# A two-layer graph network on one core: norm work one operation per gap, factor steps between halves of projections, the first two tiles ahead of the second burst

## Chip, core and metric

The kernel runs on one core of one Trainium2 chip. The metric is the device time of one execution in microseconds (us). PE is TensorE, DVE is VectorE, ACT is ScalarE, POOL is GpSimd, SP is SyncE, which here only issues DMAs.

## What is computed

The input x has 8 batches of 2048 nodes with 256 features, all in float32, and one 2048 x 2048 adjacency matrix that all batches share. Two layers follow each other.

```python
# layer 0: 4 heads of 64; the keys in 8 chunks of 256, softmax within each chunk
q, k, v = x @ Wq.T + bq, x @ Wk.T + bk, x @ Wv.T + bv
scores = clip(q kc / 8, -10, 10);  scores = where(adj == 0, -10, scores)
ctx    = sum over chunks of softmax(scores within the chunk) @ vc
x = layernorm(x + (layernorm(ctx @ Wo.T + bo + x) * gamma + beta))
# layer 1: graph attention, 4 heads of 64
Wh = x @ W;  e[i, j] = leaky_relu(s_src[i] + s_dst[j], 0.2), -inf where adj == 0
x = layernorm(x + elu(softmax over j (e) @ Wh))
```

## The kernel before

**Staging.** The adjacency matrix is turned once, during batch 0, into two tables in DRAM: clipD (int8, clip bounds of layer 0) and edgeD (bf16, the mask of layer 1). Then the kernel goes through the batches. In the loop over batch b, layer 0 of batch b and layer 1 of batch b - 1 (`lower`, called `along` where it runs) are woven together by hand[...].

**The pair loop.** A batch has 64 slots (4 query groups q x 2 head pairs x 8 chunks), taken in 32 pairs p. With QP = 8 pairs to a query group, i = p % 8 is the place in the group. In pair p, PE gets in this order: `burst(p + 1)`, four units of scores for the next pair (line 398, tile ps, 32 matmuls); one `use` of layer 1 (line 884, tile pa); `product(s0)` (line 449, tile pc); three more `use`; `product(s1)`; and in some pairs half of an output projection (line 600, `LAST_OF`) or of the layer 1 projection (line 642, `NEXT_LAST`). DVE gets: the reciprocal of the slot before (line 466, in `normalize`), the evictions of two units (line 415, tile pr), two tiles e (line 855, in `make`), the middle steps, the reciprocal of s0, two more evictions and two more tiles e. ACT takes the exponentials (line 438) and copies the products out (line 456); POOL scales and adds them up (lines 473, 475).

**The tables of steps.** The norm work of layer 0 for a group of 512 nodes is an object `Between`. Its steps are bias (line 584), shift (588), add (611), scale (617) and again (620) on DVE, and sums, squares and apply on ACT. `FIRST_OF`, `MIDDLE_OF`, `LAST_OF` and `FINALLY_OF` say at which i the current group does which step: at the head of the pair, in the middle, after the second product, and at the end. `NEXT_MIDDLE`, `NEXT_LAST` and `NEXT_FINALLY` say it for the group before. `turn_context` (line 493) transposes a block of the context on DVE. `CLOSING` says at which pair the output norm of batch b - 2 does what: load (line 956), add (959), sums, squares, factors, finish.

**PSUM.** `two_banks` gives out three tiles of two banks in turn (ps, pc, po, pw, pp, pv and others), so a tile waits for the readers of the third one before it. `one_bank` gives out two single banks, where the accumulators pa of layer 1 stand during the pair loop.

**The transition.** Between the pair loops of two batches, `order` lists the pieces: the projections of the next batch (k0, v0, q0 to k3, v3, q3; chunk g in each), the last group's norm and its layer 1 projection, the three factor steps `fs` (most, spread, rows), which turn the layer 1 scores into factors, `coming.start` (loads the first row of scores, srow), and `start_next` (burst 0 with its evictions). The tiles e of layer 1 read srow and an edge tile each (four edge buffers, three loaded ahead). All loads stand on SP's one queue in program order.

## Time and profile before

| | us |
|---|---|
| median of 3 runs | 3708.56 |
| lowest and highest run | 3708.34, 3709.61 |
| profiled execution, its own time | 3715.49 |
| span of the profiled execution | 3713.7 |
| PE busy | 3547.3 (96%) |
| DVE busy | 3055.2 (82%) |
| ACT busy | 2302.6 (62%) |
| POOL busy | 1458.7 (39%) |
| mean granted TensorE clock | 0.991 of full speed |

The span is the time from the first to the last instruction of the profiled execution; all times of single instructions and waits below are of that one execution. In a row of waits stand the total in us, how often, and the longest. In a row of the timeline stand the start, the duration, the engine, the line of the kernel, the operation, what is written and read, the shape and the count; in brackets stands how long the engine was idle before it and what released it.

### The profile page before, as it was taken

What the parts mean: (1) busy time and instruction counts of PE and PEld (TensorE: products, weight loads), DVE (VectorE), ACT (ScalarE), POOL (GpSimd) and SP (SyncE); (2) the same over time, 40 slices, a digit from 0 to 9 for tenths busy, and PEclk for the clock granted to TensorE, in tenths of its full rate; (3) what the DMA queues carried; (4) which work ended last, traced back from release to release, by engine and by line L of the source; (5) the groups of instructions that cost most, each with busy time, mean ns of one, the idle gap of its engine ahead of it and who ended that gap; (6) DMA issues with size and microseconds to landing.
All of it is one profiled execution on the core that took longest, in us unless ns stands there. A gap on an engine that the chain in (4) does not pass through costs nothing.

```text
span 3713.7 us, 169348 instructions
## 1 busy us (share of the span) xinstructions
PE 3547.3 (96%) x76884; PEld 2630.8 (71%) x76884; DVE 3055.2 (82%) x3652; ACT 2302.6 (62%) x4119; POOL 1458.7 (39%) x1259
## 2 busy tenths in 40 slices
PE   8999999999999999999999999999999999998777
PEld 5666677776777677776777767777677776775677
DVE  5886689978889699896989969988689977896787
ACT  4786456655666566665666656666566665666376
POOL 0454233333333334333433423434333333334366
PEclk9999999999999999999999999999999999999998
DMA  7764344554545455554555545555455554543432
GB/s 184 169 138 84 107 142 140 149 120 144 155 137 147 99 170 151 151 145 104 163 150 143 141 121 167 145 147 126 130 149 145 148 131 138 150 143 95 142 119 90
DMA packets 692866, 512.33 MB, mean 138 GB/s; under 512 B 429616, under 2 KB 528304, under 8 KB 692144
## 3 DMA queue, kind: packets, MB, share of 16 engines
q1 hardware_dynamic: 642144, 467.80, 46.1%
q10 hardware_dynamic: 50000, 33.70, 2.9%
q8 instruction: 601, 9.85, 1.1%
q14 instruction: 121, 0.99, 0.1%
HBM read 440.27 MB, written 61.08 MB: 135 GB/s over the span
## 4 chain that ended last, share of the span: by engine, by line
PE 65%; DVE 15%; issue 4%; ACT 2%; DMA 1%; POOL 1%; DVEq 0%; ACTq 0%; SPq 0%; POOLq 0%
PE pa L884 19%; PE pc L449 18%; PE ps L398 16%; DVE pr L415 6%; DVE e L855 5%; PE pp L342 4%; PE pw L642 3%; PE po L600 3%; PE pv L358 2%; DMA et<-edgeD 1%; DVE h L928 1%; DVE qT L493 1%; DVE xg L588 0%; DVE y L620 0%; ACT raw L456 0%
## 5 line engine op out<-in xcount | busy, mean ns | idle before, releaser
L438 ACT ACTIVATE pr<-pr 128x1024 f32<-128x1024 f32 x960 | 994.8, 1054 | 449.7 <-DVE pr L415 381.8
L415 DVE SCALAR_TENSOR_TENSOR pr<-ps,slab 128x1024 f32<-128x1024 f32 x960 | 1116.5, 1204 | 127.8 <-PE ps L398 104.2
L855 DVE SCALAR_TENSOR_TENSOR e<-srow,gd,et 128x1024 f32<-128x1024 f32 x896 | 1175.4, 1344 | 22.7 <-PE pa L884 9.0
L884 PEld LDWEIGHTS pa<-waug,e 128*64 128x64 f32 x32768 | 1014.1, 140 | 240.3 <-issue 183.4
L884 PE MATMUL pa<-waug,e 128*64 128x65 f32 x32768 | 1067.5, 224 | 61.8 <-DVE e L855 42.9
L449 PE MATMUL pc<-vaug,pr 128*64 128x65 f32 x30720 | 994.6, 222 | 48.9 <-DVE pr L415 23.3
L449 PEld LDWEIGHTS pc<-vaug,pr 128*64 128x64 f32 x30720 | 944.6, 138 | 78.2 <-DVE pr L415 40.6
L398 PE MATMUL ps<-qT,kT 64*64 64x512 f32 x8192 | 951.7, 598 | 13.5 <-DVE pr L415 10.9
L473 POOL TENSOR_TENSOR part<-raw,rd 128x512 f32<-128x512 f32 x448 | 473.5, 1057 | 1232.3 <-DVE rd L466 1228.5
L398 PEld LDWEIGHTS ps<-qT,kT 64*64 64x64 f32 x8192 | 285.4, 132 | 501.0 <-issue 272.4
L456 ACT COPY raw<-pc 128x520 f32<-128x520 f32 x512 | 302.9, 592 | 537.3 <-PE pc L449 536.0
L475 POOL TENSOR_TENSOR acc<-acc,part 128x512 f32<-128x512 f32 x448 | 593.9, 1326 | 35.2
L466 DVE RECIPROCAL rd<-raw 128x8 f32<-128x8 f32 x512 | 99.6, 194 | 195.8 <-ACT raw L456 192.1
L473 POOL TENSOR_TENSOR acc<-raw,rd 128x512 f32<-128x512 f32 x64 | 66.8, 1044 | 362.0 <-DVE rd L466 362.0
L642 PE MATMUL pw<-w_sb,x1T 128*64 128x264 f32 (+1 forms) x800 | 125.1, 392 | 6.5 <-DVE x1T L300 5.0
L600 PE MATMUL po<-wo_sb,qT 128*64 128x256 f32 (+1 forms) x912 | 120.7, 381 | 1.6 <-DVE rd L466 0.8
L342 PE MATMUL pp<-xT,wk_sb 128*128 128x512 f32 x256 | 118.8, 608 | 2.5 <-DVE xT L312 1.3
L342 PE MATMUL pp<-xT,wq_sb 128*128 128x512 f32 x256 | 117.7, 603 | 0.0
L358 PE MATMUL pv<-wv_sb,xT 128*128 128x256 f32 x512 | 117.4, 382 | 0.0
L920 ACT ACTIVATE sums<-sums,dn 128x64 f32<-128x64 f32 x448 | 117.1, 334 | 0.4 <-ACT y L564 0.4
L826 POOL TENSOR_TENSOR e<-e,et 128x1024 f32<-128x1024 f32 x42 | 90.0, 2146 | 48.4 <-ACT e L825 39.6
L642 PEld LDWEIGHTS pw<-w_sb,x1T 128*64 128x64 f32 (+1 forms) x800 | 83.7, 153 | 33.8 <-issue 5.3
(140 smaller groups left out, 2567.5 us busy)
## 6 DMA issues: line engine op xcount, KB each, us to landing
et<-edgeD SPq DMA_DIRECT2D x896, 256.0 KB, 3.5
slab<-clipD SPq DMA_DIRECT2D x256, 256.0 KB, 4.3
srow<-rowD SPq DMA_DIRECT2D x64, 512.0 KB, 5.1
xg<-in_x_dram SPq DMA_DIRECT2D x32, 512.0 KB, 5.5
x1D<-y ACTq DMA_DIRECT2D x32, 512.0 KB, 3.0
ctxD<-acc ACTq DMA_DIRECT2D x56, 256.0 KB, 3.9
ctx<-ctxD SPq DMA_DIRECT2D x224, 64.0 KB, 4.0
xp<-in_x_dram SPq DMA_DIRECT2D x224, 64.0 KB, 2.5
```

The source lines that it names most:

```text
L342: nc.tensor.matmul(pps[c], lhsT=w[:, kc, c * P : (c + 1) * P], rhs=st["xT"][:, kc, :], start=(kc == 0), stop=(kc == KC - 1),)
L398: nc.tensor.matmul(ps[z * D : (z + 1) * D, k, :], lhsT=kT[rows, hp, t * P + z * D : t * P + (z + 1) * D], rhs=qT[rows, hp, cols], start=Tr ...
L415: nc.vector.scalar_tensor_tensor(pr, ps, -CLIP, row.unsqueeze(1).to_broadcast([P, 2, CH]), op0=ALU.max, op1=ALU.min,)
L438: nc.scalar.activation(pr, pr, AF.Exp, scale=0.125)
L449: nc.tensor.matmul(pc[z * D : (z + 1) * D, k, to], lhsT=probs[s][u][:, k, i * P + z * D : i * P + (z + 1) * D], rhs=vaug[:, KT * c + u, 2 ...
L456: nc.scalar.copy(raws[s].rearrange("p k i d -> p k (i d)"), pc[:, :, : QT * D1])
L473: nc.gpsimd.tensor_mul(part, raw[:, :, :, :D], rd.to_broadcast([P, 2, QT, D]))
L475: nc.gpsimd.tensor_add(accv, accv, part)
L600: nc.tensor.matmul(po[z, k, :], lhsT=qT[:, c, t * P + z.start : t * P + z.stop], rhs=wo_sb[:, c, :], start=(c == 0), stop=(c == KC - 1),)
L642: nc.tensor.matmul(pw[z, k, : F + 2 * H], lhsT=self.x1T[:, c, u * P + z.start : u * P + z.stop], rhs=w1_sb[:, c, :], start=(c == 0), stop= ...
L855: nc.vector.scalar_tensor_tensor(e, row, self.gd[:, h, j : j + 1], self.mask(k), op0=ALU.max, op1=ALU.mult,)
L884: nc.tensor.matmul(self.pa[i // QT][z * D : (z + 1) * D, i % QT, :], lhsT=e[:, i * P + z * D : i * P + (z + 1) * D], rhs=self.waug[:, j, h ...
```

## The change

Four edits. The tables of steps: bias moves from i = 2 to 1; shift from the middle of i = 6 to the head of i = 6, the factors stay; scale moves from i = 0 of the next group to i = 7 of its own; again moves to i = 0, and the sums and squares of the second norm move one pair earlier with it; the context transpose of i = 6 moves to the head of i = 7. The closing table: all four loads stand at the batch start, and the adds are at pairs 0, 3, 1 and 7 for groups 0 to 3. The transition: `linear` takes a step to run between its two halves; the factor steps stand inside k3, after it, and inside q2, with one-bank tiles (but in the last batch); v3 comes directly ahead of `start_next`, the exponentials of pair 0 come ahead of q3, and the first two tiles of layer 1 (`coming.make` twice) come at the end of the transition. In pair 0 the two `make` that stood after burst 1 are gone.

```diff
--- before.py
+++ after.py
@@ -331,13 +331,15 @@
             else:
                 st["xT"] = transposed(st["x"], "xT", nc.vector.tensor_copy)
 
-        def linear(dst, w, bias, apart=False):
+        def linear(dst, w, bias, apart=False, between=None):
             if apart:
                 pps = [one_bank([P, CH], "pp") for _ in range(KC)]
             else:
                 pp = two_banks([P, KC, CH], "pp")
                 pps = [pp[:, c, :] for c in range(KC)]
             for c in range(KC):
+                if c and between:
+                    between()
                 for kc in range(KC):
                     nc.tensor.matmul(
                         pps[c],
@@ -370,9 +372,9 @@
         return [
             load,
             turn,
-            lambda: linear(kT, wk_sb, bk_sb),
+            lambda between=None: linear(kT, wk_sb, bk_sb, False, between),
             values,
-            lambda: linear(qT, wq_sb, bq_sb, b > 0 and g == NCH - 1),
+            lambda between=None: linear(qT, wq_sb, bq_sb, b > 0 and g == NCH - 1, between),
         ]
 
 
@@ -660,10 +662,12 @@
     FIRST_OF = {
         3: lambda o: o.add((0, 1)),
         4: lambda o: o.add((2, 3)),
+        6: lambda o: o.shift(),
     }
     MIDDLE_OF = {
-        2: lambda o: o.bias(),
-        6: lambda o: (o.a.factors(), o.shift()),
+        1: lambda o: o.bias(),
+        6: lambda o: o.a.factors(),
+        7: lambda o: o.scale(),
     }
     FINALLY_OF = {
         4: lambda o: o.a.sums(every),
@@ -675,15 +679,14 @@
         3: lambda o: o.output((2, 3)),
     }
     NEXT_MIDDLE = {
-        0: lambda o: o.scale(),
-        1: lambda o: o.again(),
+        0: lambda o: o.again(),
         3: lambda o: o.b2.factors(),
         4: lambda o: o.load(),
         5: lambda o: o.turn(),
     }
     NEXT_FINALLY = {
-        1: lambda o: o.b2.sums(every),
-        2: lambda o: o.b2.squares(every),
+        0: lambda o: o.b2.sums(every),
+        1: lambda o: o.b2.squares(every),
         3: lambda o: o.finish(),
     }
     NEXT_LAST = {
@@ -701,16 +704,17 @@
         ed = small.tile([P, H, NT], F32, tag="ed", name="ed", bufs=1)
         gd = small.tile([P, H, NT], F32, tag="gd", name="gd")
         st = {}
+        banks = one_bank if b + 1 < B else two_banks
 
         def most():
             nc.vector.tensor_reduce(top, d, AX.X, ALU.max)
-            pt = two_banks([P, CH], "pt")
+            pt = banks([P, CH], "pt")
             nc.tensor.transpose(pt[:H, :P], top, identf)
             st["most"] = small.tile([H, 1], F32, tag="most", name="most")
             nc.vector.tensor_reduce(st["most"], pt[:H, :P], AX.X, ALU.max)
 
         def spread():
-            pb = two_banks([P, CH], "pb")
+            pb = banks([P, CH], "pb")
             nc.tensor.matmul(
                 pb[:, :H],
                 lhsT=st["most"].to_broadcast([H, P]),
@@ -729,7 +733,7 @@
 
         def rows():
 
-            pr = two_banks([P, CH], "pr1")
+            pr = banks([P, CH], "pr1")
             nc.tensor.transpose(pr[: H * NT, :P], s.rearrange("p h t -> p (h t)"), identf)
             flat = small.tile([H * NT, P], F32, tag="flat", name="flat", bufs=1)
             nc.scalar.copy(flat, pr[: H * NT, :P])
@@ -1066,16 +1070,16 @@
             finish_constants()
 
     CLOSING = {
-        -1: [(0, "load", HOME), (1, "load", HOME)],
+        -1: [(0, "load", HOME), (1, "load", HOME), (2, "load", HOME_Y), (3, "load", HOME_Y)],
         0: [(0, "add"), (0, "sums")],
-        1: [(0, "squares")],
-        2: [(1, "add"), (0, "factors"), (0, "finish"), (2, "load", HOME_Y)],
-        3: [(1, "sums")],
-        4: [(1, "squares"), (3, "load", HOME_Y)],
-        5: [(2, "add"), (1, "factors"), (1, "finish")],
+        1: [(2, "add"), (0, "squares")],
+        2: [(0, "factors"), (0, "finish")],
+        3: [(1, "add"), (1, "sums")],
+        4: [(1, "squares")],
+        5: [(1, "factors"), (1, "finish")],
         6: [(2, "sums")],
-        7: [(2, "squares")],
-        8: [(3, "add"), (2, "factors"), (2, "finish")],
+        7: [(3, "add"), (2, "squares")],
+        8: [(2, "factors"), (2, "finish")],
         9: [(3, "sums")],
         10: [(3, "squares")],
         11: [(3, "factors"), (3, "finish")],
@@ -1142,6 +1146,8 @@
                 turns[0].pop(0)()
 
             hook(FIRST_OF, {})
+            if i == QP - 1:
+                turn_context(q, 0)
             if p:
                 normalize(s0 - 1)
             if more:
@@ -1151,9 +1157,6 @@
                 exps(*us[0])
                 exps(*us[1])
             if along:
-                if p == 0:
-                    for _ in range(STEP):
-                        along.make()
                 along.rest(1)
                 along.make()
                 along.use()
@@ -1169,8 +1172,6 @@
                 closing.do(p, "add", "factors")
             if i == 2 and q:
                 turn_context(q - 1, 1)
-            if i == QP // 2 + 2:
-                turn_context(q, 0)
             product(s0)
             if along:
                 normalize(s0)
@@ -1200,7 +1201,6 @@
             if p == PAIRS - 1:
                 if b + 1 < B:
                     turns[0].pop(0)()
-                group.scale()
                 group.again()
             product(s1)
             if along and more:
@@ -1260,8 +1260,9 @@
             order = [begin, early[0], *rest, l1, k0, ctx, early[2], v0, steps[0], *rest, steps[1], t1, l2, *rest]
             order += [q0, steps[2], early[3], steps[3], l3, k1, *rest, steps[4], v1, early[4], t2, q1]
             order += [steps[5], k2, steps[6], early[5], early[6], steps[7], coming.begin, v2, t3]
-            order += [lambda: [load_slab(p) for p in range(2)], steps[8], steps[9], k3, fs[0], q2, fs[1]]
-            order += [v3, fs[2], coming.start, start_next, q3, lambda: [exps(*us) for us in units_of(0)]]
+            order += [lambda: [load_slab(p) for p in range(2)], steps[8], steps[9]]
+            order += [lambda: k3(fs[0]), fs[1], lambda: q2(fs[2]), coming.start, v3, start_next]
+            order += [lambda: [exps(*us) for us in units_of(0)], q3, coming.make, coming.make]
         else:
 
             step = lower.step
```

## Prediction, made before the changed kernel ran

> **What bounds the kernel now.** I read the page first, then the waits of TensorE, then the timeline around a batch start and around one pair. A "pair" p is one turn of the loop of 32 pairs in a batch, i = p % 8.

> ```profile
> PE 3547.3 (96%) x76884; PEld 2630.8 (71%) x76884; DVE 3055.2 (82%) x3652; ACT 2302.6 (62%) x4119; POOL 1458.7 (39%) x1259
> ```

> TensorE is nearly always occupied, so only its stalls can be won. VectorE at 82% is the engine that could cause them. The waits of PE say so (total us, times, longest):

> ```profile
> PE pa L884 <- DVE e L855: 42.9, 23, 6.3
> PE pc L449 <- DVE pr L415: 23.3, 44, 1.2
> PE pc L449 <- issue: 22.5, 32, 2.3
> PE pa L884 <- issue: 11.9, 16, 1.8
> PE ps L398 <- DVE pr L415: 10.9, 23, 2.9
> PE pt L499 <- POOL acc L475: 10.8, 8, 5.6
> ```

> Three rows are VectorE being late (77 us), two are PE's own issue. The change speaks to the first kind. Where are they? At the start of batch 2 the timeline shows:

> ```profile
> 856.54 2.47 DVE L855 SCALAR_TENSOR_TENSOR e<-srow,gd,et 128x1024 f32<-128x1024 f32 x2
> ...
> 857.96 1.15 PE L884 MATMUL pa<-waug,e 128*64 128x65 f32 x32 [1.19 <-DVE e L855]
> ...
> 858.93 0.68 DVE L928 SCALAR_TENSOR_TENSOR h<-ee,sums 128x512 f32<-128x512 f32 x1
> ...
> 861.92 1.22 DVE L959 TENSOR_TENSOR h<-h,x1g 128x1024 f32<-128x1024 f32 x1
> ...
> 864.49 1.70 PE L449 MATMUL pc<-vaug,pr 128*64 128x65 f32 x51 [0.71 <-DVE pr L415]
> ```

> The reader is to see that the first tile e is made only after two evictions of burst 1, PE waits 1.19 us for it, and VectorE, then behind, costs 0.71 us more at pc. The waits asked in a window over each batch start repeat it: 1.2 us in all seven (batches 1 to 7), 0.7 us in the six that also close an older batch (0.6 in one).

> Inside a batch, pairs 14 and 15 of batch 3 on VectorE:

> ```profile
> 1474.24 0.71 DVE L928 SCALAR_TENSOR_TENSOR h<-ee,sums 128x512 f32<-128x512 f32 x1
> ...
> 1477.41 1.21 DVE L588 TENSOR_TENSOR xg<-xg,beta_sb 128x1024 f32<-128x1024 f32 x1
> 1478.55 0.70 DVE L493 STREAM_TRANSPOSE qT<-ctx 128x512 f32<-128x512 f32 x1
> 1479.18 0.16 DVE L466 RECIPROCAL rd<-raw 128x8 f32<-128x8 f32 x1
> ...
> 1490.44 0.20 DVE L466 RECIPROCAL rd<-raw 128x8 f32<-128x8 f32 x1 [1.09 <-ACT raw L456]
> ```

> and on PE:

> ```profile
> 1480.48 2.31 PE L449 MATMUL pc<-vaug,pr 128*64 128x65 f32 x64 [0.25 <-DVE pr L415]
> 1482.72 2.81 PE L398 MATMUL ps<-qT,kT 64*64 64x512 f32 x24
> 1485.68 1.09 PE L398 MATMUL ps<-qT,kT 64*64 64x512 f32 x8 [0.15 <-DVE pr L415]
> ```

> Pair 15 has no norm work, and there VectorE idles 1.09 us before the reciprocal of slot s0: that is the middle gap, and it holds one operation of 1.2 us. Pair 14 put 2.2 us into it (factors, shift, context transpose), after an L928, so the second product starts late, and the next burst breaks after 24 of 32 matmuls because the first eviction is late. From the starts of the 32 ps matmuls a pair lasts 11.21 us undisturbed, 12.94 with half an output projection, 12.99 with half of the layer 1 projection.

> [...] the trace has 1207 to 1218 for bias, shift and the closing add, so spreading doesn't shrink them. [...] scale and again (L617, L620) average 1352 and 1422 ns against about 1220 alone, and two e take 2.47 us alone and 2.93 beside the POOL work in pair 14. [...] the page has an instruction queue of 601 packets and 9.85 MB, 16.4 KB each, so the issue stalls of PE can depend on DMA traffic.

> **The change part by part.**

> *First two tiles made at the end of the transition.* Nothing is added: the same two L855 (2.47 us) and their edge loads are moved. VectorE has the room: it idles 2.81 us (851.46 to 854.27) before burst 1. The row srow that they read landed at about 853 before; its store is now issued a projection (3.7 us) earlier, because the rows step sits between the halves of q2, so it lands near 848. PE's 1.19 goes seven times, and VectorE, 2.5 us further on, no longer holds pc: 7 x 1.19 + 5 x 0.7 + 0.6 = 12.4. If the cover fails (srow late), up to 8.3 of it is lost. Late next would be nothing in pair 0.

> *Factor steps between halves.* The three small PE pieces (0.27, 0.38, 0.27 us) stay. Each waits for a short chain on VectorE and ScalarE. The longest is the exponential of s, which before was ready 1.5 us after pb began (841.61 to 843.13); half of q2 covers 1.8 us, k3's activations run in that time too. So cost 0, bounds 0 to +0.5 a transition. With one-bank tiles the bursts no longer wait for the copy of pv (burst 0 takes 3.87 us, others 3.66): 7 x 0.2 = 1.5 gained. The exponentials of pair 0 ahead of q3 on ScalarE delay only q3's own copies, due 4 us later.

> *Scale at i = 7, again and the sums one pair earlier.* At the last pair the scale leaves the crowded stretch before the final reciprocal, on whose chain POOL and the context transposes wait (about 0.5 us per transition). Taken: half of 7 x 0.47 = 1.6; bounds 0 to 3.3.

> *One operation per gap.* Over the minimum periods the excess in batches 1 to 7 is: pair 10, 7.5 us; 14, 5.6; 15, 4.0; 18, 3.2; 22, 3.1; 26, 2.7; 30, 2.3: 28.4 together. After it bias stands in i = 1, the transposes in i = 2 and at the head of i = 7, the shift at the head of i = 6. A head position has little room: 0.2 us of waiting before the eviction and 0.43 until the fourth unit needs its bank (in pair 14 eviction 1 ended about 1473.1, the fourth unit was due at 1473.55). So the shift at the head of pair 14 should cost 1.21 - 0.63 = 0.58, pair 15 with two operations about the same, pair 10 some 0.3; pairs 22 and 30 follow a layer 1 half (1.78 us of cover) and cost nothing. Left: 7 x 1.45 = 10; saved 18. No plain pair of this trace shows an operation at its head, so I take two thirds, 12; bounds 3 and 20.

> *Closing adds.* Adds leave pairs 2, 5, 8, where they stood with the factors. Excess after those, of VectorE's kind, is about 4.4 us in six batches; 3.5 taken, bounds 0 and 5. Pair 7 now has an add and a transpose, within the tolerance.

> *Loads 2 and 3 at the batch start.* On SP's queue 1 MB more stands ahead of slab 2 and of the sixth and seventh edge tile; SP also waits for tile 0 before these loads. Where four such loads went together (kT<-x1D) they landed 9.8 us after issue in the median. Issued at 853 to 855, they end by about 863, the sixth tile by 864; it is needed near 864.5. Cost: 1 taken, bounds 0 and 12 (2 us in six batches). In return pairs 2 and 4 lose their loads. PE's issue stalls: 0 taken, -10 to +10.

> **Sum** on the profiled execution (span 3713.7, its own time 3715.5): 12.4 + 1.5 + 1.6 + 12 + 3.5 - 1 = 30.0, a span near 3683.7. The median of the runs, 3708.56, is 5.1 below that span; the same step from it gives **3678.6**.

> **Rivals.** (1) *Only the batch start gains*: the heads stall as much as the doubled gaps did, since the sum of VectorE's work over i = 6 to 2 is the same (6.6 us against some 5 of slack). Then 12.4 + 1.5 = 14: 3694.5. For it: the slack sum; against it: pairs 15, 23 waste their gap today. (2) *No change*: the MB of extra loads lands while pa and pc consume instructions fastest, and the issue stalls (34 us in two rows) double: 3708. (3) *Slower*: the queue at the batch start. If the four loads hold slab 2 and the edge tiles so long that six batches lose over 6.3 us each, 38 us are lost against the 30 gained, and beyond that it is slower; with 8 us each, 3727. That needs loads at about half the rate at which four landed in 9.8 us, so it is unlikely. That the change does nothing is excluded by the fixed 1.19 unless srow is late.

> **Chances.** Forecast 0.56, rival 1 0.24, rival 2 0.11, rival 3 0.09. Some 0.2% (7.4 us) is what a measurement of this kernel can tell. Faster 0.80, same 0.11, slower 0.09. The range takes the bounds of the gains (48 us at best) and rival 1 with some loss on the queue: 3660 to 3706.

> **What would show it.** Right: pa's wait of 1.19 gone in all seven batch starts; the pc wait of 0.7 gone; pairs 22, 26, 30 at 12.99, 12.94; pair 14 broken after 24 matmuls of its burst (the shift), no longer at pc. Wrong: DVE e or pr waiting for et or slab in pairs 0 and 1; more issue waits at PE; pairs 15 and 23 worse than before by over 0.6.

## The result, and the profile after

| | median us | beside it: kernel before | ratio (95% interval) |
|---|---|---|---|
| changed kernel | 3672.8 | 3708.45 | 0.9909 (0.9896 to 0.9922) |
| the same, on another chip | 3683.4 | 3718.2 | 0.9910 (0.9892 to 0.9928) |

The changed kernel is 0.9% faster: 35.7 us, where 30 were forecast. Its profiled span is 3674.4 us, 39.3 below that of before. One execution of the run loads_early, described below, took 4498.5 us at a granted clock of 0.741, and its ratio leaves it out. The page's line of engines, and the waits of PE (a row with "issue" is time in which PE waited for nothing that the profile shows; it is called an issue stall below):

```profile
PE 3529.9 (96%) x76884; PEld 2627.9 (72%) x76884; DVE 3043.1 (83%) x3652; ACT 2302.7 (63%) x4119; POOL 1437.2 (39%) x1259
```

```profile
PE pa L888 <- DVE e L859: 30.6, 16, 4.6
PE pc L451 <- issue: 26.3, 27, 2.6
PE pa L888 <- issue: 20.6, 17, 2.3
PE ps L400 <- DVE pr L417: 13.2, 22, 2.0
PE pt L501 <- POOL acc L477: 10.4, 8, 6.3
PE pc L451 <- DVE pr L417: 9.7, 8, 1.2
```

The same work is done (the counts agree), and what went is waiting. PE's three rows of waits for VectorE fell from 77.1 to 53.5 us. The two issue rows rose from 34.4 to 46.9, and the start of batch 2 shows where (start, duration, engine, line, count, idle time before):

```profile
837.05 2.47 DVE L859 SCALAR_TENSOR_TENSOR e<-srow,gd,et 128x1024 f32<-128x1024 f32 x2
...
838.58 3.66 PE L400 MATMUL ps<-qT,kT 64*64 64x512 f32 x32
838.71 2.08 SPq L960 DMA_DIRECT2D x1g<-x1D  x4
...
842.17 1.15 PE L888 MATMUL pa<-waug,e 128*64 128x65 f32 x32
...
845.02 2.15 PE L888 MATMUL pa<-waug,e 128*64 128x65 f32 x66
...
848.90 1.09 PE L888 MATMUL pa<-waug,e 128*64 128x65 f32 x29 [1.73 <-issue]
```

The two tiles e begin 5.1 us before PE wants the first of them and both are ready 2.7 us before, and the old waits of 1.19 and 0.7 us are gone. But in the middle of the next run of pa, PE stands for 1.73 us with nothing missing except its own instructions. The four loads x1g are in flight then; the trace has them landing from 842.8 to 848.7. This happens in pair 0 of all six batches that close an older one (2 to 7), with idle times of 1.15 to 2.57 us. Pair 0 had 13.4 us there before; it has 12.6 to 14.9 now. In batch 1, which closes nothing, it fell from 12.47 to 11.21, the undisturbed time.

Inside a batch, the heads of pairs 14 and 15 in batch 1, PE and VectorE rows together:

```profile
564.66 2.81 PE L400 MATMUL ps<-qT,kT 64*64 64x512 f32 x24
565.75 1.21 DVE L590 TENSOR_TENSOR xg<-xg,beta_sb 128x1024 f32<-128x1024 f32 x1
...
568.23 1.09 PE L400 MATMUL ps<-qT,kT 64*64 64x512 f32 x8 [0.76 <-DVE pr L417]
...
576.87 2.81 PE L400 MATMUL ps<-qT,kT 64*64 64x512 f32 x24
578.59 0.70 DVE L495 STREAM_TRANSPOSE qT<-ctx 128x512 f32<-128x512 f32 x1
...
580.53 1.09 PE L400 MATMUL ps<-qT,kT 64*64 64x512 f32 x8 [0.85 <-DVE pr L417]
```

Both bursts break after 24 of 32 matmuls: the operation at the head of the pair (shift on L590, context transpose on L495) holds back the eviction that the fourth unit waits for. Pair 14 lost its stall at the second product and got this one.

**Where the 39.3 us of the profile went**, from the starts of the bursts: pairs 1 to 9 of batches 1 to 7 (closing moves among them) 13.9; pairs 10, 14, 15, 18, 22, 26 together 11.2; pair 30 with the transition 2.4; burst 0 no longer waiting for pv 1.4; pair 0 only 1.2; the start of batch 0, whose code is the same in both, 5.0; the rest 4.2. The 5.0 count as chance: from burst 0 to burst 1 of batch 0 alone, the traces of all the runs below take from 9.7 to 14.2 us.

### The profile page after: what moved, and what is told of

It reads as the page before. It is cut to its first block, busy times and chain, and to the rows that moved or that the text cites. A ratio compares the mean times of both kernels' runs of the same rounds, so it can differ in the third digit from the quotient of the medians.

```text
span 3674.4 us, 169302 instructions
## 1 busy us (share of the span) xinstructions
PE 3529.9 (96%) x76884; PEld 2627.9 (72%) x76884; DVE 3043.1 (83%) x3652; ACT 2302.7 (63%) x4119; POOL 1437.2 (39%) x1259
## 3 DMA queue, kind: packets, MB, share of 16 engines
q8 instruction: 601, 9.85, 1.1%
## 5 line engine op out<-in xcount | busy, mean ns | idle before, releaser
L475 POOL TENSOR_TENSOR part<-raw,rd 128x512 f32<-128x512 f32 x448 | 477.5, 1066 | 1282.3 <-DVE rd L468 1277.9
L400 PE MATMUL ps<-qT,kT 64*64 64x512 f32 x8192 | 950.3, 597 | 14.3 <-DVE pr L417 13.2
L475 POOL TENSOR_TENSOR acc<-raw,rd 128x512 f32<-128x512 f32 x64 | 66.8, 1043 | 362.2 <-DVE rd L468 362.2
L360 PEld LDWEIGHTS pv<-wv_sb,xT 128*128 128x128 f32 x512 | 95.9, 190 | 20.2 <-issue 7.2
```

The source lines that it names most:

```text
L360: nc.tensor.matmul(pv[:, u, :], lhsT=st["xT"][:, kc, u * P : (u + 1) * P], rhs=wv_sb[:, kc, :], start=(kc == 0), stop=(kc == KC - 1),)
L400: nc.tensor.matmul(ps[z * D : (z + 1) * D, k, :], lhsT=kT[rows, hp, t * P + z * D : t * P + (z + 1) * D], rhs=qT[rows, hp, cols], start=Tr ...
L475: nc.gpsimd.tensor_mul(part, raw[:, :, :, :D], rd.to_broadcast([P, 2, QT, D]))
```

## Experiments

Ratios are to the kernel before, run beside each on the same chip; medians of different sets of runs are not comparable, since the kernel before had 3715.4, 3718.2 and 3704.6 us in the three sets. The excess is what pair 0 takes above its undisturbed 11.21 us, summed over batches 1 to 6. Batch 1 closes nothing, and batch 7, which does, is not in this sum.

| run | median us | ratio (95% interval) | excess of pair 0 over 11.21, batches 1 to 6, us |
|---|---|---|---|
| kernel before | - | 1 | 12.2 |
| steps_only | 3697.4 | 0.9955 (0.9942 to 0.9967) | 12.2 |
| closing_only | 3710.5 | 0.9988 (0.9980 to 0.9996) | 16.1 |
| transition_only | 3698.0 | 0.9954 (0.9941 to 0.9967) | 2.4 |
| makes_only | 3714.0 | 0.9989 (0.9980 to 0.9998) | 8.2 |
| changed kernel (after_again) | 3683.4 | 0.9910 (0.9892 to 0.9928) | 9.5 |
| loads_early | 3671.8 | 0.9880 (0.9864 to 0.9896) | 0.0 |
| shift_middle5 | 3678.5 | 0.9898 (0.9881 to 0.9915) | 10.6 |
| both | 3666.7 | 0.9863 (0.9849 to 0.9877) | 0.1 |
| no_stores | 3636.5 | 0.9814 (0.9793 to 0.9834) | 0.0 |
| stores_split | 3639.4 | 0.9825 (0.9804 to 0.9847) | 0.0 |

The theory: VectorE's lateness is what the change removes, and the closing loads, moved and doubled, hold back PE's instruction fetch in pair 0. The rival: the stalls of pair 0 have a cause of their own and would come with any faster start.

### The three parts alone

steps_only: the kernel before with the new tables and the moved transpose.

> The kernel before with the new tables of steps and the moved context transpose alone. Theory (one operation per gap removes VectorE's stalls at the doubled gaps, the heads of pairs 14 and 15 give some back): pairs 10, 18, 22, 26, 30 lose their excess (about 19 us in batches 1 to 7), pairs 14 and 15 stall about 1 us each in their bursts; 10 to 14 us faster, 3694 to 3698. Rival (the sum of VectorE's work decides, not its place): within 4 us of the kernel before.

Measured: 0.9955, 16.7 us (12 to 22 by the interval), somewhat more than the 10 to 14 of the theory. The waits ps <- DVE pr rose from 10.9 to 18.0 us while pc <- DVE pr fell from 23.3 to 14.0: the doubled gaps are gone and the heads stall. The theory holds in kind, and the rival (within 4 us) falls.

closing_only: `CLOSING` of the change in the kernel before.

> The kernel before with the new closing table alone (four loads at the batch start, adds away from the factors). Theory (the four loads hold back PE's instruction fetch while pa and pc of pair 0 run): VectorE's 4 us after pairs 2 and 5 go, issue stalls of 1 to 2 us appear in pair 0 of batches 2 to 7, partly beside the VectorE stalls that are there anyway; between 6 us faster and 4 us slower. Rival (the loads cost nothing, the stalls of pair 0 come from something else): 5 to 9 us faster with no issue stall in pair 0.

Measured: 0.9988, 4.5 us, within the theory's range of time. Pair 0 became slower, from 13.4 to 14.4 and 14.9 us, in three of the six closing batches, and stayed within 0.1 us in the others. But the cause is not the expected one. Batch 4:

```profile
1754.09 1.28 DVE L855 SCALAR_TENSOR_TENSOR e<-srow,gd,et 128x1024 f32<-128x1024 f32 x1 [1.40 <-DMA et<-edgeD]
...
1755.42 1.15 PE L884 MATMUL pa<-waug,e 128*64 128x65 f32 x32 [0.70 <-DVE e L855]
```

The edge tile stands behind the four loads on SP's queue and lands late, so VectorE waits 1.40 us for it, and PE then waits for VectorE, here and once more at pc (1.28 us). VectorE waits so in just the three batches that became slower (0.89, 1.40 and 1.38 us). Over batches 1 to 7, PE's waits for VectorE in pair 0 rose from 12.5 to 14.9 us, and of issue stalls there is one of 0.3. In this kernel the loads cost what the third rival of the prediction named, the queue at the batch start, in a small size; the stall of instructions in pair 0 was not seen.

transition_only: `linear` with `between`, the new order with its two early tiles, and the one-bank tiles.

> The kernel before with the transition alone (factor steps between halves, one-bank tiles, first two tiles at its end); tables of steps and closing loads as before. Theory (the pair 0 gain of 1.9 us was taken by the two added loads): pair 0 of batches 2 to 7 falls from 13.4 to about 11.3 us as in batch 1; with 4 us from the transition itself 16 to 19 us faster, 3689 to 3692. Rival (PE's fetch stalls in pair 0 as soon as VectorE no longer holds it, with two loads as well): pair 0 stays near 13, 5 to 7 us faster, 3702.

Measured: 0.9954, 17.1 us; pair 0 at 11.2 to 11.6 us in six of seven batches, 13.2 in one. The one of 13.2 is an issue stall of 1.76 us, beside two loads; otherwise the gain of pair 0 is there. The parts sum to 1.03% and the whole is 0.9%, which the intervals do not tell apart. The column of pair 0 does: the closing moves add 3.9 us to it in the kernel before (12.2 to 16.1), and the change, which has the transition, the closing moves and the steps (these leave pair 0 at 12.2), stands 7.1 us above transition_only (2.4 to 9.5).

makes_only: only the two early tiles.

```diff
-                if p == 0:
-                    for _ in range(STEP):
-                        along.make()
...
-            order += [..., q3, lambda: [exps(*us) for us in units_of(0)]]
+            order += [..., q3, lambda: [exps(*us) for us in units_of(0)], coming.make, coming.make]
```

> The kernel before with the first two tiles made at the end of the transition and nothing else; the factor steps stand where they stood, so the first row lands near 853 us in batch 2 instead of 3.7 us earlier. Theory (the early makes alone carry the pair 0 gain): pair 0 at 11.2 to 11.7 us, 12 to 14 us faster. Rival (they need the earlier row: VectorE waits for srow some 1.2 us ahead of burst 1's eviction): half of it, pair 0 near 12.3, 5 to 8 us faster.

Measured: 0.9989, 4.2 us, below both ranges. Its timeline at the start of batch 2:

```profile
849.46 2.48 DVE L855 SCALAR_TENSOR_TENSOR e<-srow,gd,et 128x1024 f32<-128x1024 f32 x2 [1.03 <-ACT qT L350]
...
853.13 1.09 PE L398 MATMUL ps<-qT,kT 64*64 64x512 f32 x8 [0.23 <-DVE pr L415]
...
859.90 1.21 PE L884 MATMUL pa<-waug,e 128*64 128x65 f32 x34 [0.87 <-issue]
```

The row srow lands at 849.37, so VectorE waits for it 1.03 us (the profile names ACT, which was done at 849.17), evicts burst 1 late (from 851.86), and PE's burst breaks. The edge load behind the first tile stands on SP's queue ahead of the closing loads, which so go out at 851.14, one microsecond after burst 1 began, and an issue stall follows. Pair 0 keeps 8.2 of its 12.2 us of excess. The early tiles pay in full only with the factor steps moved as well, which brings the row forward (transition_only).

### The loads

loads_early: the four loads ahead of v3. Shown is the line of `order`; for it, the object that does the closing is also made at the end of the batch before.

```diff
-q2(fs[2]), coming.start, v3, start_next]
+q2(fs[2]), coming.start, load_closing, v3, start_next]
```

> The changed kernel with the four closing loads issued right after the load of the first row, ahead of v3, while the DMA engines are idle and PE runs projections. Theory (the loads hold back the instruction fetch in pair 0): the issue stalls of 1.3 to 2.8 us in pair 0 of batches 2 to 7, 12 us in the profile, go; 3659 to 3663. Rival (the stall has another cause, such as where the instruction blocks end): same as the changed kernel, 3670 to 3676.

Measured: 0.9880 (0.9864 to 0.9896), which by the ratios is 0.3% or 11 us better than the changed kernel. As a median, 3671.8 us lies in the rival's range; but the kernel before was 7 us slower beside this run than beside the first run of the changed kernel (3715.4 against 3708.45), from which these ranges are reckoned. As ratios to the 3708.45, the theory said 0.9867 to 0.9877 and the rival 0.9896 to 0.9913, so the measured interval holds the theory's range and only touches the rival's. The trace decides: pair 0 is 11.21 us in all seven batches.

```profile
836.65 2.52 SPq L960 DMA_DIRECT2D x1g<-x1D  x4
...
852.89 2.97 PE L888 MATMUL pa<-waug,e 128*64 128x65 f32 x96
```

They go out where the DMA share of the changed kernel was 0.00 (834 to 838 us) and land from 842.0 to 846.4, by the start of burst 1, and the run of pa that broke after 66 matmuls is whole. The theory stands and the rival falls: same instructions on PE, same megabytes, other time.

after_again: the changed kernel a second time.

> The changed kernel itself, beside the two that build on it. Every theory: 0.988 to 0.992 of the kernel before; in the profile issue stalls of 1 to 3 us in pair 0 of batches 2 to 7 again if the loads cause them, in other places if they are chance.

The stalls of pair 0 came again in the same six batches (pair 0 takes 12.9 to 13.3 us there), each at the very same instruction of PE as in the first trace, so they are not chance. The two issue rows together have 39.7 us here and 46.9 in the first trace, so such sums differ by some 7 us from one execution to the next.

### The heads

shift_middle5: no operation at the head of pairs 6 and 7.

```diff
-        6: lambda o: o.shift(),          (FIRST_OF)
+        5: lambda o: o.shift(),          (MIDDLE_OF)
-            if i == QP - 1:
-                turn_context(q, 0)
+            if i == QP // 2 + 2:           (behind the middle steps)
+                turn_context(q, 0)
```

> The changed kernel with no operation at the head of pairs 6 and 7: shift in the middle of i = 5, context transpose in the middle of i = 6 beside the factors. Theory (a head has 0.63 us of room, a middle gap 1.1 us): the breaks after 24 matmuls in pairs 14 and 15, about 1 us each in seven batches, go, and pairs 21 and 29 bear transpose and shift under the layer 1 half; 9 to 14 us faster than the changed kernel, ratio to the kernel before 0.987 to 0.989. Rival (VectorE's sum decides): the stalls move to pairs 16 to 18 or 21 and 29; within 4 us of the changed kernel.

```profile
568.76 3.66 PE L400 MATMUL ps<-qT,kT 64*64 64x512 f32 x32
...
579.97 4.01 PE L400 MATMUL ps<-qT,kT 64*64 64x512 f32 x32
```

In the profile the heads are free (batch 1: the burst of pair 14 is whole, that of pair 15 takes 0.35 us more), and pairs 14 and 15 together fell from 11.1 us of excess (after_again) to 1.3 over batches 1 to 6. But pairs 21 and 29, which now have transpose and shift in one gap, wait more for VectorE (4.4 us in batches 1 to 7, where after_again has 1.4). The issue rows are 47.6 us, 7.9 above after_again, which is about the difference between the two traces of the changed kernel. The median is 4.9 us better, and the ratio's interval overlaps that of the changed kernel. So the gain in pairs 14 and 15 is shown, its forecast size of 9 to 14 us was missed, and a gain in the whole is not separated from none.

both: early loads and free heads.

> The changed kernel with the closing loads ahead of v3 and with no operation at the head of pairs 6 and 7. Theory: both gains add, 20 to 26 us faster than the changed kernel, ratio to the kernel before 0.984 to 0.986. Rival (the fetch stalls grow where VectorE no longer holds PE): 8 to 14 us, ratio about 0.988.

Measured: 0.9863, 16.7 us better than the changed kernel beside it and clear of its interval; between the two expectations, short of the theory's sum. Issue stalls of 40.1 us remain.

### What else delays the instructions

In version both, the excess of pairs 3, 6, 9 and 12 is 20.9 us over the six closing batches. These are the pairs with an output store, as here pair 3 of batch 2:

```profile
880.04 2.06 ACT L566 ACTIVATE x1g<-h,off_c,rs_c 128x256 f32<-128x256 f32 x4
...
882.13 0.39 SPq L969 DMA_DIRECT2D out_dram<-x1g  x1
882.57 0.50 SPq L388 DMA_DIRECT2D slab<-clipD  x1
...
883.16 7.05 SPq L805 DMA_DIRECT2D et<-edgeD  x4
...
889.22 2.08 PE L451 MATMUL pc<-vaug,pr 128*64 128x65 f32 x62 [1.27 <-issue]
```

SP's queue holds the store until apply has ended (882.10); slab and edge tiles follow in a bunch, 0.44 us behind the store and from 1.03 us on; PE stops at 887.95, 5.8 us after the store.

no_stores: these 24 stores left out, so that their part of the output stays unwritten.

> The version with early loads and free heads, with the 24 output stores of batches 0 to 5 inside the pair loop left out (their results are not written). Theory (bulk transfers ahead of the instruction blocks make PE's issue stalls): the stalls after pairs 3, 6, 9 and 12, where a 512 KB store stands at the head of the pair (about 18 us over batches 1 to 6 in the profile), fall to below 5 us; ratio 0.982 to 0.984. Rival (issue stalls come from the place in the instruction stream or from the edge tiles alone): pairs 3, 6, 9, 12 keep over 12 us, ratio 0.986.

Measured: 0.9814; the four pairs keep 2.9 us, where the theory said below 5 and the rival over 12. The theory holds.

stores_split: two halves, the second a pair later. `half(u)` sends half of the store, and `delayed` is added to `outgoing` at the next pair; these lines are not shown.

```diff
-            outgoing.append(lambda: nc.sync.dma_start(out=by_node(out, self.b, self.g), in_=o))
+            outgoing.append(lambda: half(0))
+            delayed.append(lambda: half(2))
```

> The version with early loads and free heads, with every output store sent as two halves of 256 KB, the second one pair later. Theory: each half meets fewer queued bytes, the stalls of pairs 3, 6, 9 and 12 fall by a third to a half; ratio 0.983 to 0.986, and pairs 4, 7, 10, 13 rise a little. Rival (what counts is the total of bytes in the stretch): same as without the split, 0.986 to 0.987.

Measured: 0.9825, a little more than expected; the four pairs keep 6.1 of 20.9 us, and pairs 4, 7, 10 and 13 did not rise: their excess together fell from 11.2 to 6.1 us. PE's issue waits, in version both, without stores, and with split stores:

```profile
PE pc L451 <- issue: 24.7, 33, 2.2
PE pa L888 <- issue: 15.4, 15, 2.4
```

```profile
PE pa L888 <- issue: 12.8, 11, 2.0
PE pc L451 <- issue: 10.6, 13, 1.7
```

```profile
PE pa L890 <- issue: 13.5, 15, 2.6
PE pc L453 <- issue: 10.7, 15, 2.0
```

From 40.1 to 23.4 and 24.2 us. The split version moves as many bytes as version both, so the total of bytes alone does not make the stalls. A half store also waits for only two of the four apply instructions, so it leaves SP's queue earlier (in pair 3 of batch 2, 2.7 us after the start of the pair instead of 3.7). Whether the size of one store or the bunching behind the wait counts more was not separated. This version does the whole computation and is the fastest one: 1.75% under the kernel before, and its interval lies below that of the changed kernel.

## Why the prediction was right, and which terms were not

**Pair 0, forecast 12.4, got 1.2.** The mechanism was right: VectorE's stalls there, which made an excess of 14.4 us over batches 1 to 7, are all gone. The step that failed is the one on the closing loads. It asked only whether slab and edge tiles come in time (in five of the six batches VectorE waited 0.25 to 1.28 us for one, and PE never for VectorE) and put the issue stalls at 0 with a range of 10 either way. They took 13.2 us back in six batches. The working had noticed that SP waits for the first tile e ahead of these loads, and did not follow it: the wait put them at 838.71, beside the start of burst 1 at 838.58. Before, they stood 4 us ahead of burst 1, which began at 853.11:

```profile
849.09 0.93 SPq L956 DMA_DIRECT2D x1g<-x1D  x2
```

So they fell into pa and pc. There PE runs 96 matmuls in 2.97 us, where a burst has 32 in 3.66, so it uses up its instructions almost four times as fast. Rival 2 named this mechanism; the issue rows rose by 12.5 us, about a third of the doubling that would have undone the gain. Of the signs of being wrong, more issue waits at PE came, and a tile e that waits for its edge tile, the latter at no cost.

**Steps, forecast 12, got 13.6** with pair 30 and the transition. The head of pair 14 was put at 0.58 us and cost 1.0 in four of seven batches (in the other three pair 13 had lost time before it); pair 15 about 1.0 in most. The room at a head had been put too high: its 0.2 us of waiting was gone too, since two e beside POOL ended late (2.70 and 3.33 us in the batch shown, where the pair of 570.11, with POOL idle, took 2.47). Pairs 18, 22, 26, 30 lost their stalls as forecast.

**Transition.** Burst 0 gave 1.4 (forecast 1.5), the factor steps cost nothing. The 1.6 for the scale was wrong: the context transposes still wait for POOL, 10.4 us in eight (10.8 before), and at the six inner transitions 0.53 us each instead of 0.48. That wait fell to 7.4 us in two only in the versions with shift and context transpose off the heads. The transpose stood at the head of pair 31 itself, so it probably used up what the early scale won; the two moves were not tried apart.

**Closing and issue, forecast 2.5 and 0.** Pairs 1 to 9 gave 13.9. In idle time of PE that is 8.1 us less waiting for VectorE (8.5 before, 0.4 after) and 1.7 less of issue stalls (17.8 and 16.1). Alone, the closing moves leave 2.4 of the 8.5 and the transition leaves 3.8, so the two shares are not told apart. closing_only puts the table's own effect at 4.5 us in all, and issue stalls change their size between traces, so the 13.9 holds chance too.

**Batch 0.** 5.0 us of the span's 39.3 lie at the start, ahead of the second burst, where the code is the same; the forecast had nothing there, and the medians, 35.7 apart, carry less of it.

The total came within 6 us because the loss in pair 0 was met by gains that had been put low or at nothing, some of them chance. The direction follows from the mechanism; that the total came so close is luck. What the forecast said of the gaps held: one operation fits the middle gap, and a head has little room. Its best case does not come out of its own terms: the upper bounds add up to 42.2 us without issue stalls and 52.2 with them, not to 48; the lower end of the range, 3660, would move by about 6 us at most.

## What to carry to other kernels

When a stall on one engine is taken away, ask what that engine consumes next, its instructions included: here the same four loads cost pair 0 nothing while PE ran matmuls of 256 and 512 columns (loads_early), and 2 us a batch when it ran 65-column ones (the changed kernel, 13.2 us in six). On SP's queue a transfer that waited delayed everything behind it: the closing loads went out only at 838.71, behind an edge load that waited for a tile e until 838.35, and a slab and four edge tiles from 882.57 on, behind a store. Try to place bulk loads ahead of such a wait, which gave 11 us here, and to split bulk stores, which took the issue stalls from 40.1 to 24.2 us. One operation per gap worked here only where the gap was (the heads of pairs 14 and 15 cost about 1.0 us each): measure the idle time before the instruction that follows, at the very place to which the operation is moved.

## What was not expected of the hardware

The traces show it without exception. Counted along PE's instructions, all 94 issue stalls over 0.15 us in the traces of the kernel before (50) and of the changed kernel (44) stand at one place of such a block, give or take one instruction, and none elsewhere. In the changed kernel 25 of them are over 0.8 us. Each of these ends 1.3 to 1.8 us after a packet of the instruction queue has landed. That packet took as long as the others, about 0.97 us, but it began late: in the median 3.1 us after PE had passed the boundary before, against 0.65 us at the boundaries without such a stall. So the block of instructions is not moved more slowly beside the loads; it starts to move later. loads_early shows that the loads are what delays it in pair 0; by what step they do so is not shown by the traces.

Beside 2 MB of loads, the stalls in pair 0 of the changed kernel were 1.15 to 2.57 us each, and splitting 24 stores went with 16 us less of issue stalls (40.1 to 24.2).
